# Layer 2's attention set-up: keys and queries from one product, six diffusions made ahead, first blocks' first sums by VectorE

## The chip, the cores and the metric

One core of one Trainium2 chip runs the whole four-layer network in one launch. The metric is the time of one execution in device microseconds (us). Engines: PE is the matrix engine (TensorE), PEld its weight loads, DVE VectorE, ACT ScalarE, POOL GpSimd, SP SyncE.

## The reference, cut to what matters

Layer 2 gets X (4096 x 256) and S (the 0/1 adjacency). It takes two steps; each makes a nucleus (top-p) attention and a diffusion, and then multiplies both by small weights:

```python
def top_p_attention(X, W1, W2, W3):
    q = X @ W1.T @ W2.T            # 4096 x 64
    k = X @ W3.T                   # 4096 x 64
    probs = softmax(q @ k.T)       # 4096 x 4096
    ...                            # keep the largest until their sum reaches 0.9
    return A / max(A.sum(-1), 1e-12)
R = (S + I) / row sums
for n in range(2):
    A  = top_p_attention(Xa, W1, W2, W3)
    Xf = R @ Xf                    # diffusion
    Xa = A @ Xa                    # attention
    Z  = Z + Xf @ U1[n].T + Xa @ U2[n].T
h = X + Z                          # then a layer norm with gain and shift
```

## The kernel before

Rows are worked in 32 blocks of 128. For a block, `scores` makes the logits (PE) and their exponentials (ACT) into one of three large buffers `e`, guesses the cut and takes a first sum above it; `nucleus` searches the cut on VectorE and masks the exponentials; `attention` transposes the masked block and multiplies it by X; `diffuse` multiplies the adjacency by X; `close` applies the small weights. `work` and `psum` are buffer pools; the kernel's builder orders the instructions of each engine itself, from the program order and the buffers.

```python
# keys(src), one group of four blocks; ps_tp has two PSUM buffers
for g in range(NB // 4):
    self.transposed(psum, work, src[:, 4 * g:4 * g + 4, :], None, out=xT)
    pk = ...; matmul(pk, w3 twice, xT)                 # keys, 2 products of 512 columns (L711)
    nc.vector.tensor_copy(kT[half, ...], pk[half, :])
    pq = ...; matmul(pq[:A], w1, xT)                   # queries, first half of the chain (L718)
    nc.scalar.copy(q1, pq[:A])
    pr = ...; transposes of kT                         # keys by rows (L722)
    pq = ...; matmul(pq, w2 twice, q1)                 # queries, second half (L727)
    nc.scalar.copy(qs[:, g * 512:(g + 1) * 512], pq)
# ... moments of the keys (L732)
for b in range(NB):                                    # the spreads: 32 rounds (L737)
    matmul(pg[:, :2 * A + 1], qs[:A, block b], mom)
    nc.scalar.copy(g, pg[:, :2 * A + 1])
    nc.vector.tensor_copy(mean[:, b:b + 1], g[:, 2 * A:])
    nc.vector.scalar_tensor_tensor(..., accum_out=hvar[:, b:b + 1])
# ... (cut)

# in scores(b): the first sum, on ACT
for s in range(2):
    for i, f in ((0, AF.Relu), (2, AF.Sign)):
        nc.scalar.activation(ja, e[:, s * HALF:(s + 1) * HALF], f, bias=nc1, accum_out=fs[:, i + s:i + s + 1])

# the order of the blocks, once per step
keys(X)
for b in range(-2, NB):
    if b >= 0:
        attention(att[:, 0], stage.pop(b)[0], rs.pop(b))
        close(step, b, (twos.pop(b), att))
    if b + 2 < NB:
        stage[b + 2] = scores(b + 2, ABOVE[step])
    if 0 <= b + 1 < NB:
        rs[b + 1] = nucleus(*stage[b + 1], evals=1 + step)
        diffuse(dif[:, 0], b + 1)
        # ... (in step 0 the diffusion is split and stored for step 1)
```

## Time and profile before

| | before |
|---|---|
| median of the runs beside the changed kernel | 5093.11 us (5086.0 to 5099.69, 4 runs) |
| profiled execution | 5087.6 us, mean granted PE clock 0.953 |
| layer 1's last product ends | 2077 us |
| step 0 of layer 2 ends (last attention scaling) | 3363 us |
| step 1 ends | 4734.5 us |
| DVE's first search starts in step 0, step 1 | 2202.2, 3477.2 us |

The windows of the whole steps serve as a ledger: length, then busy us of PE, PEld, DVE, ACT, POOL (with the number of instructions), then granted clock, DMA share and GB/s.

```profile
2078.00:3363.00 1285.00, 1204.81 (x5320) 855.43 (x5320) 971.81 (x2800) 802.55 (x1927) 0.86 (x2) 0.97 0.24 77
3363.00:4734.50 1371.50, 1222.11 (x5332) 858.71 (x5332) 1173.36 (x3494) 861.39 (x2148) 64.37 (x124) 0.96 0.23 72
```

Step 0 is PE's (idle 80 of 1285 us), step 1 is shared: DVE works 1173 and PE 1222 of 1371.5. In rows of PE, one product of the code is often two records (the two products of L711 are `x4`).

### The profile page before, as it was taken

Reading aid. Unit: us, or ns where it says so; the run is one execution under the profiler, and the core shown is the slowest. Engines: PE = TensorE matmul, PEld = TensorE weight load, DVE = VectorE, ACT = ScalarE, POOL = GpSimd, SP = SyncE. Lnnn points to the kernel's source line nnn. Section 1 sums busy time; section 2 is a strip of 40 time slices with the busy share of each in tenths; the row PEclk is TensorE's granted clock in tenths of the full one; section 3 lists DMA queues with packets and bytes.
Section 4 is the critical chain, followed back from the end, with each engine's and each line's share of the span. In section 5 each row is a group of like instructions: output and inputs, shape, how many; then the busy total and the mean of one; then the engine's idle time right before and its main releaser. Section 6 shows DMA issues by size and latency. Waiting matters only on the chain. (4 is left out here: it accounts for less than half of the span.)

```text
span 5087.6 us, 72483 instructions
## 1 busy us (share of the span) xinstructions
PE 4404.3 (87%) x25899; PEld 3464.9 (68%) x25900; DVE 3399.8 (67%) x8018; ACT 2871.7 (56%) x5755; POOL 458.5 (9%) x807
## 2 busy tenths in 40 slices
PE   6799977776777489969999999995999989989799
PEld 4699967776777378547767767753666666666677
DVE  4422228887888722377878787836989999899322
ACT  4333349997999410276666666636676676665111
POOL 3344420000000121000000000000000000000000
PEclk6899989998999799979999999997999999999899
DMA  4499982233232259502222222241112211211566
GB/s 151 158 337 348 340 330 96 96 102 141 96 102 96 80 163 309 181 24 89 69 88 69 88 69 88 71 163 39 62 62 62 80 62 61 81 62 60 183 228 201
DMA packets 338490, 659.76 MB, mean 130 GB/s; under 512 B 74048, under 2 KB 150720, under 8 KB 328896
## 3 DMA queue, kind: packets, MB, share of 16 engines
q1 hardware_dynamic: 189824, 436.29, 26.2%
q10 hardware_dynamic: 117568, 117.98, 7.0%
q0 software_dynamic: 30720, 100.69, 5.2%
q8 instruction: 209, 3.42, 0.3%
q14 instruction: 169, 1.38, 0.1%
HBM read 490.46 MB, written 164.36 MB: 129 GB/s over the span
## 5 line engine op out<-in xcount | busy, mean ns | idle before, releaser
L1073 PE MATMUL ps_a<-X,aT 128*128 128x256 f32 x4096 | 970.6, 390 | 52.3 <-ACT aT L1070 52.2
L1073 PEld LDWEIGHTS ps_a<-X,aT 128*128 128x128 f32 x4096 | 768.2, 192 | 308.4 <-ACT aT L1070 167.2
L254 PE MATMUL acc<-gm,gt 128*128 128x198 bf16 x8192 | 745.9, 250 | 255.4 <-DVE gt L249 243.8
L247 ACT ACTIVATE sg<-lpb,lc 128x1024 bf16<-128x1024 f32 x832 | 870.9, 1135 | 119.4 <-DVE gt L249 78.9
L254 PEld LDWEIGHTS <-gt 128*128 128x128 bf16 x8192 | 692.2, 98 | 308.9 <-DVE gt L249 286.4
L385 PE MATMUL pz<-src,ar 128*128 128x264 f32 x4096 | 549.7, 294 | 48.7 <-ACT src L342 34.1
L249 DVE TENSOR_TENSOR gt<-sg,na 128x4096 bf16<-128x4096 bf16 x208 | 474.2, 2286 | 164.2 <-ACT sg L247 164.2
L385 PEld LDWEIGHTS pz<-src,ar 128*128 128x128 f32 x4096 | 522.9, 194 | 70.3 <-ACT src L342 44.6
L143 PE MATMUL ps_r<-XD,adj_piece 128*128 128x512 f32 x2048 | 501.7, 397 | 29.6 <-DMA adj_piece<-adjs 28.9
L1070 ACT COPY aT<-ps_tp 128x512 f32<-128x512 f32 x512 | 276.8, 583 | 420.9 <-PE ps_tp L1068 413.7
L822 ACT ACTIVATE ja<-e,nc 128x2048 bf16<-128x2048 f32 x256 | 511.0, 1996 | 1.0 <-DVE e L959 0.4
L143 PE MATMUL ps_adj<-XD,adj_piece 128*128 128x512 f32 x2048 | 494.2, 399 | 16.1 <-DMA adj_piece<-adjs 11.0
L764 PE MATMUL ps_logit<-kT,q 64*128 64x512 f32 x1024 | 442.2, 654 | 53.3 <-ACT e L768 51.1
L143 PEld LDWEIGHTS ps_r<-XD,adj_piece 128*128 128x128 f32 x2048 | 382.2, 189 | 131.4 <-DMA adj_piece<-adjs 50.2
L143 PEld LDWEIGHTS ps_adj<-XD,adj_piece 128*128 128x128 f32 x2048 | 385.4, 190 | 99.2 <-DVE XD L115 11.7
L852 DVE SCALAR_TENSOR_TENSOR v<-e,c 128x4096 bf16<-128x4096 f32 x96 | 429.5, 4474 | 1.1
L76 POOL TENSOR_SCALAR ln_var<-ln_mv 128x1 f32<-128x1 f32 (+1 forms) x144 | 49.5, 344 | 4139.3 <-DVE kept L935 1469.6
L959 DVE SCALAR_TENSOR_TENSOR e<-e,edge 128x256 f32<-128x256 f32 x1024 | 415.8, 479 | 1.4
L377 ACT ACTIVATE nb<-a 128x512 bf16<-128x512 f32 x256 | 158.1, 630 | 348.8 <-DMA a<-in_adjt_dram 255.6
L912 DVE MAX8 cand<-v 128x8 f32<-128x256 f32 x1024 | 349.1, 412 | 3.4
L1068 PE MATMUL ps_tp<-ident,e 128*128 128x128 f32 x2048 | 274.3, 276 | 52.9 <-DVE e L959 52.9
L1068 PEld LDWEIGHTS ps_tp<-ident,e 128*128 128x128 f32 x2048 | 242.9, 142 | 90.9 <-DVE e L959 61.9
(285 smaller groups left out, 4869.8 us busy)
## 6 DMA issues: line engine op xcount, KB each, us to landing
adj_piece<-adjs SPq DMA_DIRECT2D x256, 512.0 KB, 5.5
adj_piece<-adjs SPq DMA_DIRECT2D x512, 256.0 KB, 3.5
a<-in_adjt_dram SPq DMA_DIRECT2D x256, 256.0 KB, 5.7
adjs<-ar POOLq DMA_DIRECT2D x256, 256.0 KB, 5.6
na<-nad SPq DMA_DIRECT2D x64, 1024.0 KB, 6.4
nad<-nb POOLq DMA_DIRECT2D x128, 256.0 KB, 5.1
lpb<-lpd ACTq DMA_DIRECT2D x32, 512.0 KB, 5.0
gmd<-gb ACTq DMA_DIRECT2D x64, 198.0 KB, 2.1
```

Source lines behind the costliest of these rows:

```text
L143: nc.tensor.matmul(ps, a[:, k, :], rhs(jc).rearrange("p s d -> p (s d)"), start=(jc == 0 and own is None), stop=(jc == self.NB - 1))
L247: nc.scalar.activation(sg[:, k, :], lpb, AF.Sign, bias=lc[:, jc, h:h + 1])
L249: nc.vector.tensor_tensor(*flat, ALU.is_gt)
L254: nc.tensor.matmul(acc[:, q, :6 * C1], gt[:, k, q * P:(q + 1) * P], gm[:, jc, hh, :], start=(jc == 0 and q % 2 == 0), stop=(jc == NB - 1 a ...
L385: nc.tensor.matmul(pz[q][:, t, :W], ar[:, q, k, :], src[:, jc, t, s], start=(jc == 0 and s == 0), stop=(jc == NB - 1 and s == 1))
L764: nc.tensor.matmul(pl[:, s, :], q[s * A:(s + 1) * A, :], kT[s * A:(s + 1) * A, c * 512:(c + 1) * 512], start=True, stop=True)
L822: nc.scalar.activation(ja, e[:, s * HALF:(s + 1) * HALF], f, bias=nc1, accum_out=fs[:, i + s:i + s + 1])
L852: nc.vector.scalar_tensor_tensor(junk, e, c, e, op0=ALU.is_ge, op1=ALU.mult, accum_out=S)
L912: nc.vector.max(cand[:, 8 * j:8 * j + 8], v[:, k * 256:(k + 1) * 256])
L959: nc.vector.scalar_tensor_tensor(ec, ec, edge[:, j:j + 1], ec, op0=ALU.is_ge, op1=ALU.mult)
L1068: nc.tensor.transpose(pt[:, k * P:(k + 1) * P], e[:, jc * P:(jc + 1) * P], self.ident)
L1073: nc.tensor.matmul(pa[:, :D], aT[:, k * P:(k + 1) * P], X[:, jc, :], start=(jc == 0), stop=(jc == NB - 1))
```

## The change

Its intent: PE does less for the keys, and the work that waits nowhere else (the diffusions) is moved to where PE stood idle, between the keys and block 0's attention.

```diff
 # one-time: W1 and W2 multiplied into one weight, keys and queries side by side in wkq
+for c in range(2):
+    matmul(pt[:, :A], w1[:, c, :], aw2)
+    for s in range(2):
+        nc.vector.tensor_copy(wkq[:, c, s, 1 - s, :], pt[:, :A])
+        nc.vector.tensor_copy(wkq[:, c, s, s, :], aw3[:, c, :])
 # the 32 additions of the layer norm's shift leave the start of step 0 ...
-    nc.vector.tensor_add(xl, X[:, b, :], lnb)
-    nc.scalar.dma_start(xd[b, :, 2, :], xl)
 # ... and go into step 0's closes
+    nc.vector.tensor_add(xb[:, 1], xb[:, 0], affine)
+    nc.scalar.dma_start(xd[at(b), :, 2, :]..., xb[:, 1])
 # the splits of X for step 0's diffusions: from ahead of the keys to behind them
-    self.split(XD[:, b], X[:, b, :])        # at the start
+    self.split(XD[:, b], X[:, b, :])        # after keys(X), if step == 0
 # keys (kT is now centred at their end, ahead of the spreads and not after them)
-    pk from w3, pq from w1, q1, pq from w2 (above)
+    matmul(pk, wkq[:, c, s], xT)            # keys in one half, queries in the other
+    nc.vector.tensor_copy(kT[half, ...], pk[half, :])
+    here = qs[other, g * 512:(g + 1) * 512]
+    nc.scalar.copy(here, pk[other, :])
 # spreads: four blocks to a PSUM bank, the mean taken out of the moments beforehand
-for b in range(NB): ...
+for g in range(NB // 4):
+    four matmuls into pg
+    nc.scalar.copy(t, pg[:, :, :A])
+    nc.vector.tensor_mul(t, t, pg[:, :, A:])
+    nc.vector.tensor_reduce(hvar[:, 4 * g:4 * g + 4], t, AX.X, ALU.add)
 # first sum
+if b < 2:
+    S1 = evaluate("S1", e, c1)              # one DVE instruction over 4096
+else: (ACT, as before)
 # order
+found = keys(X)
+e = scores(0)
+spreads(*found)
+stage = {0: guessed(e, 0, ABOVE[step])}
+rs = {0: nucleus(*stage[0], evals=1 + step)}
+for k in range(EARLY):                      # EARLY = 6
+    if k in (2, 4):
+        stage[k // 2] = guessed(scores(k // 2), k // 2, ABOVE[step])
+    nc.scalar.dma_start(ahead[k], diffusion(step, k)[:, 0])
 # blocks 0 to 5 load their diffusion from ahead; later blocks make it as before
```

## The prediction

> **What bounds the kernel now.** The page's busy shares (PE 87%, DVE 67%, ACT 56%) average four layers, and its chain of waits reaches back over only 6% of the span, all in layer 3. So I read layer 2 by stretches. In the trace, layer 1's last product ends at 2078 us, the first pass of layer 2 (step 0) ends at 3363, the second (step 1) near 4740. I cut each pass into its head (to the end of block 0's attention) and a long middle of 24 blocks.
>
> The windows view; columns after the length are busy us of PE, PE weight loads, DVE, ACT, POOL, then the granted PE clock, DMA share and GB/s:
>
> ```profile
> 2078.00:2255.00 177.00, 125.80 (x494) 69.25 (x495) 93.98 (x331) 90.97 (x219) 0.86 (x2) 0.82 0.20 67
> 2469.00:3333.00 864.00, 839.46 (x3756) 609.98 (x3754) 695.23 (x1934) 571.82 (x1373) 0.00 (x0) 1.00 0.25 79
> 3363.00:3545.00 182.00, 123.67 (x505) 64.72 (x505) 84.00 (x301) 92.35 (x233) 0.00 (x0) 0.84 0.33 108
> 3775.00:4702.00 927.00, 853.01 (x3744) 616.42 (x3745) 862.33 (x2530) 608.62 (x1522) 51.89 (x96) 0.98 0.21 67
> ```
>
> Per block, by division by 24: step 0 takes 36.0 us, of which PE works 35.0 and DVE 29.0, so PE bounds it. Step 1 takes 38.6 us, DVE works 35.9 and PE 35.5, so DVE bounds it with PE just behind. The heads are different: 177 and 182 us, with PE idle for 51 and 58.
>
> The timeline of PE shows where the idle lies. First step 0, then step 1:
>
> ```profile
> 2199.91 3.60 PE L764 MATMUL ps_logit<-kT,q 64*128 64x512 f32 x8 [10.13 <-ACT e L768]
> ...
> 2216.34 3.78 PE L764 MATMUL ps_logit<-kT,q 64*128 64x512 f32 x8 [9.80 <-ACT e L768]
> 2232.89 1.97 PE L1068 MATMUL ps_tp<-ident,e 128*128 128x128 f32 x8 [12.76 <-DVE e L959]
> ```
>
> ```profile
> 3523.73 1.97 PE L1068 MATMUL ps_tp<-ident,e 128*128 128x128 f32 x8 [26.56 <-DVE e L959]
> ```
>
> PE waits for exponentials that stand behind the first sums on ACT, then for the first mask (L959). And one group of the keys, of eight:
>
> ```profile
> 3385.16 1.93 PE L718 MATMUL ps_tp<-e,aw 128*64 128x512 f32 x4
> 3387.02 0.46 PE L722 MATMUL ps_tp<-ident,kT 64*128 64x64 f32 x4
> 3387.41 0.45 PE L732 MATMUL ps_a<-e 128*64 128x65 f32 x4
> 3387.82 1.12 PE L727 MATMUL ps_tp<-e,aw 64*128 64x512 f32 x2
> 3388.87 0.65 PE L96 MATMUL ps_tp<-ident,X 128*128 128x128 f32 x4
> 3389.45 0.45 PE L732 MATMUL ps_a<-e 128*64 128x65 f32 x4
> 3389.83 0.66 PE L96 MATMUL ps_tp<-ident,X 128*128 128x128 f32 x4
> 3390.32 2.02 PE L711 MATMUL ps_tp<-e,aw 128*128 128x512 f32 x4
> ```
>
> PE has no gap there: the keys are PE-bound at 7.1 us a group (the group before starts L711 at 3383.21).
>
> [...] granted clock 0.82 and 0.84 in the heads, 1.00 in step 0's middle. [...] the trace has DVE standing at L1084 behind an unfinished diffusion for 95.4 us in step 0's middle.
>
> **The change part by part.**
>
> *Keys and queries from one product.* W1 and W2 are multiplied once, so L718 and L727 go: from the starts above, 1.86 us (3385.16 to 3387.02) and 1.05 us (3387.82 to 3388.87) a group. 7.1 - 2.9 = 4.2 us a group; over 8 groups 23 us per step, all on the path. Copies per group stay below that: ACT three at 0.58 us, DVE 0.68 and 0.42. The one-time product costs some transposes and small copies, about 3 us, while step 0 waits for weights anyway.
>
> *Removed at the start of step 0.* The 32 additions of the shift with their stores go into step 0's closes. In the trace ACT's first key copy came at 2093.65, after such a store, 13 us after its transposes. I count 5 us of earlier start. The price is one DVE addition (0.42 us) and one store per block in step 0, where DVE has 7 us of room a block.
>
> *Spreads.* Before: 32 products, each with its ACT copy of 0.27 and three small DVE instructions, took from 2157.3 to 2174.5, 17 us; in step 1 3434.0 to 3451.5. After: four blocks share a bank, eight rounds. A round is four products at 0.32 us (L737's x4 rows, two products in 0.64 us), 1.3 us: about 11 us, so 6 saved. The scores of block 0 are put ahead of them in program order, but its exponentials need one of the three large buffers, and all three are the keys' scratch until the spreads have read it. Only the first products into PSUM can go ahead, so I count no more than the shorter spreads and the earlier centring of kT.
>
> *First sums by DVE for blocks 0 and 1.* Four ACT passes of 2.0 us plus readouts (2189.1 to 2198.3, 9.2 us) become one DVE instruction of 4.47 us (the row of L852). For block 0 both are on the path: 4.5 saved, and block 1's passes no longer delay its exponentials.
>
> *Six diffusions ahead.* One costs (182.6 + 11.7) / 24 = 8.1 us of PE, from the middle's rows of L143 and L137. One already ran beside the keys. So five more, 40 us of PE, move from the first blocks into the hole.
>
> *Step 0's sum*, by PE, since PE bounds it from the keys on. Work removed: 23 + 6 = 29. Idle removed: the head had 51; I leave 20 (8 while weights land, 3 while kT is centred, 9 between diffusions, which share one PSUM bank), so 31. Together 60 us. DVE does not get in the way: with masks starting some 50 us earlier and 28.5 us a block it stays ahead of PE's 27 us blocks plus backlog.
>
> *Step 1's sum*, by DVE. Its first search started at 3477.2. After: keys end 23 earlier; from keys to the first exponential 21.1 us become about 16; from there to the first search 22.6 become about 14.5 (exponentials 5, Z and first cut 4, DVE's sum 4.7, second cut 0.8). So the search starts 36 us earlier. DVE then carries one first sum more (4.5) and saves idle: it stood idle about 5 us in 3477:3545 and about 20 us in the ten blocks to 3775 where PE was the reason. I count 12 of these. 36 - 4.5 + 12 = 44 us.
>
> 60 + 44 = 104 us. I take off 6 for friction that such a reordering has had no chance to tune out: **98 us, 4998 us**.
>
> **The rivals.**
> 1. *Diffusions stall on their one bank.* Each must be read out by ACT and then DVE (L1083, L1084) before the next begins, and DVE may be inside a pass of 4.47 us. For: the 95.4 us above. Against: PE has three blocks' logits (7 us each) to put between. If every gap is 4 us longer, 24 us a step come back: about 5045.
> 2. *Diffusions stand in front of the first attention.* About 90 us of PE work (logits 21, spreads 11, diffusions 49, gaps 9) follow the keys, while the first mask is ready after about 50. Then block 0's large buffer is freed late and block 3's scores with it. In step 0 this costs nothing, PE being busy; in step 1 DVE would run dry between blocks 2 and 3, for 10 to 20 us: about 5012.
> 3. *The new stores hold ACT.* [...] Against: ACT waits for transposes 213 us in step 0's middle, 9 us a block, so it has room. If 1 us a block reaches PE: about 5030.
> 4. *Better:* PE has almost no idle left after the keys, and with the diffusions gone from blocks 1 to 5 step 1 runs at DVE's 36 us: some 25 us more, 4973.
>
> **Range and chances.** The key saving is nearly certain, and rivals 1 to 3 can hardly all strike. 8 in 10: 4960 to 5042. The 2% line lies at 4994, four us under my figure, so it is close to even: faster 0.45, within 2% 0.53, slower 0.02.
>
> **What would show it.** L711 rows 4 to 4.5 us apart in the keys; no L718 or L727. First L959 mask some 50 us earlier after each step's start. L143 rows of six diffusions between the keys and the first L1068, with PE gaps under 3 us, and the granted clock near 1.0 there. Blocks 1 to 5 of step 0 some 28 to 30 us apart by the attention's scaling, of step 1 about 36. It is wrong if the holes are filled yet the first attentions start no earlier, if DVE waits at L1084 inside the first search, or if blocks beyond the sixth grow longer than 36.0 and 38.6 us.

## More of the kernel before

In step 1 the blocks do not come evenly: their lengths repeat with a period of nine, from about 34 to about 46 us. The order of PE's rows in the trace shows what goes with it: in seven blocks of nine the diffusion stands ahead of the block's transposes, then once after seven of the eight transposes of the first round, then once after all eight (the 34 us block), and then it is in front again and the long blocks come.

## The result, and the profile after

The changed kernel takes 5002.82 us in the median (4998.48 to 5005.48, 4 runs) against 5093.11 for before. The ratio is 0.9822, 95% interval 0.9805 to 0.9839. (Ratios here are the mean time of one kernel's runs over that of the other's of the same rounds, so not quite the ratio of the medians.) That is "within 2%" at the edge, and 5 us from the predicted 4998. (The prediction's 98 us and 4998 us belong to a before of 5096; against the 5093 measured here the gain is 90 us.) A second set of runs, the unaltered kernel run again later, gave 5000.18 us and 0.9819 (0.9806 to 0.9832). All outputs are right.

The same ledger of the changed kernel:

```profile
2078.00:3307.40 1229.40, 1181.06 (x5282) 848.21 (x5282) 977.22 (x2736) 776.99 (x1878) 0.86 (x2) 0.99 0.25 81
3307.40:4646.60 1339.20, 1203.16 (x5288) 864.66 (x5288) 1182.72 (x3421) 836.23 (x2092) 67.93 (x124) 0.96 0.23 75
```

Step 0 is 55.6 us shorter: PE works 23.8 less (1204.81 - 1181.06) and is idle 31.9 less (80.2 against 48.3). Step 1 is 32.3 us shorter: DVE works 9.4 more and is idle 41.7 less (198.1 against 156.5). The rest of the program is 3 us shorter.

The windows of the head and middle of step 0, and of the head of step 1, to be set beside those of before:

```profile
2078.00:2225.00 147.00, 128.07 (x621) 87.60 (x622) 92.46 (x240) 68.47 (x180) 0.86 (x2) 0.95 0.45 138
2225.00:2377.00 152.00, 140.53 (x613) 99.13 (x611) 132.61 (x379) 103.07 (x249) 0.00 (x0) 0.97 0.08 24
2420.00:3282.00 862.00, 850.57 (x3768) 615.99 (x3767) 700.39 (x1946) 564.07 (x1356) 0.00 (x0) 1.00 0.26 83
3307.00:3473.00 166.00, 136.78 (x628) 97.70 (x626) 104.75 (x266) 70.17 (x185) 0.00 (x0) 0.89 0.59 189
```

The head of step 0 ends 30 us earlier with 19 us of PE idle (the prediction left 20) and the granted clock at 0.95 instead of 0.82. Blocks 1 to 5 then take 152 us, five at 30.5, where they took 178. From block 7 on the middle is as before, 36 us a block.

The keys of step 1, one group of eight, in PE's timeline (start, length, line, and in brackets the idle time before and who ended it):

```profile
3337.16 1.98 PE L725 MATMUL ps_tp<-e,wkq 128*128 128x512 f32 x4
...
3340.53 1.09 PE L96 MATMUL ps_tp<-ident,X 128*128 128x128 f32 x8 [0.16 <-ACT e L729]
3341.46 0.40 PE L740 MATMUL ps_a<-e 128*65 128x65 f32 x4
3341.91 1.98 PE L725 MATMUL ps_tp<-e,wkq 128*128 128x512 f32 x4
3343.74 0.40 PE L740 MATMUL ps_a<-e 128*65 128x65 f32 x4
3344.69 0.46 PE L732 MATMUL ps_tp<-ident,kT 64*128 64x64 f32 x4 [0.55 <-DVE kT L727]
```

A group takes 4.76 us, not 4.2: two rows now carry a wait, 0.55 us for VectorE's copy of the keys and 0.15 us for ACT's copy of the queries. In the group of before that the prediction shows there was none.

The spreads of the changed kernel, from their first to their last product, in step 0 and in step 1 (the windows view):

```profile
2139.98:2149.15 9.17, 9.17 (x70) 7.96 (x67) 5.40 (x14) 2.61 (x7) 0.00 (x0) 1.00 0.09 29
```

```profile
3363.90:3377.55 13.65, 13.65 (x66) 13.65 (x68) 5.89 (x14) 2.60 (x7) 0.00 (x0) 0.50 0.65 233
```

PE has no gap in either; what differs is the granted clock, 1.00 and 0.50. It fell in step 1 from 1.00 to 0.50 at 3361 us, at the end of the keys; the longest wait in the 34 us before was 0.55 us.

The end of the hole in step 0, then the same place in step 1:

```profile
2194.09 0.50 PE L137 MATMUL ps_r<-XD,identr 128*128 128x512 f32 x1 [2.03 <-DVE dif L1115]
2194.43 7.50 PE L143 MATMUL ps_r<-XD,adj_piece 128*128 128x512 f32 x32
2203.09 1.62 PE L1099 MATMUL ps_tp<-ident,e 128*128 128x128 f32 x8 [1.16 <-DVE e L990]
```

```profile
3436.96 0.44 PE L1099 MATMUL ps_tp<-ident,e 128*128 128x128 f32 x2 [0.93 <-DVE e L990]
...
3444.51 2.07 PE L1104 MATMUL ps_a<-X,aT 128*128 128x256 f32 x4 [4.20 <-ACT aT L1101]
3446.20 0.81 PE L137 MATMUL ps_r<-XD,identr 128*128 128x512 f32 x1
3446.81 8.92 PE L143 MATMUL ps_r<-XD,adj_piece 128*128 128x512 f32 x32
3455.57 2.75 PE L1104 MATMUL ps_a<-X,aT 128*128 128x256 f32 x12
```

In step 0 the waits for the first mask (12.76 us before) and between diffusions have become 1 to 2 us. In step 1 the wait of 26.56 us has become 0.93, but then two things stand inside block 0's attention: a wait of 4.20 us for ACT, which was in its four half passes of block 2's first sum, and the sixth diffusion, 9.4 us long. So although the first mask comes 31.2 us earlier in the step, block 0's attention ends only 16.4 us earlier; the following five blocks then run at 34.6 us each (before 38.0) and recover 17 more, and block 6, where diffusions return, costs 48.6 us and gives 9 of them back.

The rows after such waits show one thing more. `L1104` x16 takes 3.72 us in its usual state. After waits in the changed kernel, and then at the first of these places in its second run:

```profile
2409.18 3.72 PE L1104 MATMUL ps_a<-X,aT 128*128 128x256 f32 x16 [1.80 <-ACT aT L1101]
...
3895.03 3.72 PE L1104 MATMUL ps_a<-X,aT 128*128 128x256 f32 x16 [3.06 <-ACT aT L1101]
...
4242.66 6.64 PE L1104 MATMUL ps_a<-X,aT 128*128 128x256 f32 x16 [3.57 <-ACT aT L1101]
```

```profile
2408.48 5.41 PE L1104 MATMUL ps_a<-X,aT 128*128 128x256 f32 x16 [1.80 <-ACT aT L1101]
```

In the changed kernel the sixteen products took 3.72 us after 3.06 us of idle and 6.64 us after 3.57 us, where the trace has a granted clock of 0.50 from 4242.7 to 4246.0 us. But the length of the wait just before does not settle it: the same 1.80 us left the rate in one run of the kernel and not in the other. Over layer 2 in the traces of before and of the changed kernel, such rows of sixteen took 3.72 us after each of the 14 waits of 1.34 to 1.98 us, 5.38 us after one of 2.68 us, and 5.1 to 6.7 us after each of the six waits of 3.19 us or more; but also 5.10 and 5.87 us after waits of 1.22 and 0.81 us. After the waits of 2.68 us and more, the slower rows cost 1.4 to 3.0 us beside the wait itself; what decides was not studied.

### The profile page after: what moved, and what is told of

Same layout as the page of the kernel before. It is cut to its first block, busy times and chain, and to the rows that moved or that the text cites. A ratio compares the mean times of both kernels' runs of the same rounds, so it can differ in the third digit from the quotient of the medians.

```text
span 4996.8 us, 72143 instructions
## 1 busy us (share of the span) xinstructions
PE 4366.1 (87%) x25817; PEld 3469.1 (69%) x25818; DVE 3415.4 (68%) x7880; ACT 2819.7 (56%) x5645; POOL 461.8 (9%) x807
## 5 line engine op out<-in xcount | busy, mean ns | idle before, releaser
L1104 PE MATMUL ps_a<-X,aT 128*128 128x256 f32 x4096 | 975.4, 391 | 62.8 <-ACT aT L1101 62.3
L1104 PEld LDWEIGHTS ps_a<-X,aT 128*128 128x128 f32 x4096 | 771.0, 193 | 321.9 <-ACT aT L1101 177.7
L385 PE MATMUL pz<-src,ar 128*128 128x264 f32 x4096 | 553.6, 296 | 48.6 <-ACT src L342 34.8
L860 ACT ACTIVATE ja<-e,nc 128x2048 bf16<-128x2048 f32 x240 | 478.9, 1996 | 0.8 <-DVE e L990 0.6
L787 PE MATMUL ps_logit<-kT,q 64*128 64x512 f32 x1024 | 448.9, 646 | 12.9 <-ACT e L791 12.6
L806 DVE SCALAR_TENSOR_TENSOR v<-e,c 128x4096 bf16<-128x4096 f32 x100 | 447.4, 4474 | 3.7 <-ACT c L834 2.8
L1099 PE MATMUL ps_tp<-ident,e 128*128 128x128 f32 x2048 | 276.7, 276 | 35.3 <-DVE e L990 35.2
L939 DVE SCALAR_TENSOR_TENSOR v<-e,hi 128x2048 f32<-128x2048 f32 x128 | 301.1, 2352 | 2.2
```

Source lines behind the costliest of these rows:

```text
L385: nc.tensor.matmul(pz[q][:, t, :W], ar[:, q, k, :], src[:, jc, t, s], start=(jc == 0 and s == 0), stop=(jc == NB - 1 and s == 1))
L787: nc.tensor.matmul(pl[:, s, :], q[s * A:(s + 1) * A, :], kT[s * A:(s + 1) * A, c * 512:(c + 1) * 512], start=True, stop=True)
L806: nc.vector.scalar_tensor_tensor(junk, e, c, e, op0=ALU.is_ge, op1=ALU.mult, accum_out=S)
L939: nc.vector.scalar_tensor_tensor(v, ec, hi, ec, op0=ALU.is_lt, op1=ALU.mult, accum_out=sb[:, s:s + 1])
L1104: nc.tensor.matmul(pa[:, :D], aT[:, k * P:(k + 1) * P], X[:, jc, :], start=(jc == 0), stop=(jc == NB - 1))
```

## The experiments

Layers 0 and 1 are the same code in all kernels, yet layer 1's last product ended between 2070 and 2087 us over the profiled executions. So step 0 is counted below from its own first keys product, and step 1 from the end of step 0; both ends are the last attention scaling of the step. Times of the profiled executions, in us:

| kernel | step 0: block 0 | block 10 | end | step 1: block 0 | block 10 | end | blocks 11 to 28 against changed | median of runs | ratio to before (95%) |
|---|---|---|---|---|---|---|---|---|---|
| before | 160.2 | 519.1 | 1268.3 | 182.4 | 571.8 | 1371.4 | +33.3 | 5093.1 | 1 |
| changed | 131.8 | 469.1 | 1214.4 | 166.0 | 533.8 | 1339.2 | 0 | 5002.8 | 0.9822 (0.9805-0.9839) |
| changed, again | 131.3 | 467.6 | 1211.1 | 166.3 | 535.4 | 1342.3 | +3.8 | 5000.2 | 0.9819 (0.9806-0.9832) |
| no diffusion ahead | 128.1 | 487.8 | 1235.3 | 153.2 | 543.3 | 1347.1 | +2.4 | 5025.2 | 0.9871 (0.9856-0.9886) |
| first sums on ACT | 140.3 | 475.7 | 1223.1 | 173.9 | 542.8 | 1354.1 | +9.2 | 5020.6 | 0.9868 (0.9853-0.9883) |
| old keys | 159.9 | 513.8 | 1259.2 | 175.9 | 547.0 | 1359.6 | +15.5 | 5061.9 | 0.9941 (0.9926-0.9956) |
| spreads first | 127.3 | 464.5 | 1209.6 | 166.4 | 534.1 | 1341.0 | +2.4 | 4993.0 | 0.9813 (0.9800-0.9826) |
| keys and spreads only | 138.1 | 497.9 | 1251.3 | 166.2 | 555.6 | 1352.7 | +16.8 | 5048.2 | 0.9920 (0.9905-0.9935) |
| five in step 1 | 127.4 | 464.0 | 1209.7 | 159.0 | 531.7 | 1343.9 | +0.1 | 5002.1 | 0.9826 (0.9813-0.9840) |
| five, third sum on DVE | 127.6 | 460.3 | 1212.9 | 148.8 | 527.7 | 1340.8 | -4.4 | 5000.1 | 0.9825 (0.9810-0.9840) |
| four in step 1 | 127.0 | 463.6 | 1210.2 | 158.2 | 523.8 | 1333.0 | -9.3 | 4991.1 | 0.9806 (0.9793-0.9819) |
| four, keys staggered | 130.3 | 471.2 | 1215.6 | 153.0 | 520.1 | 1327.9 | -13.3 | 4997.8 | 0.9814 (0.9800-0.9828) |
| old keys, five in step 0 | 151.4 | 495.6 | 1242.4 | 175.1 | 546.1 | 1355.3 | +12.9 | 5044.3 | 0.9912 (0.9896-0.9927) |
| three in step 1 | 127.7 | 464.9 | 1209.8 | 152.0 | 526.9 | 1340.7 | -7.1 | 5002.3 | 0.9821 (0.9808-0.9835) |

The two profiles of the changed kernel differ by 3.3 us in step 0 and 3.1 us in step 1, and the two runs with old keys, whose step 1 is the same code, by 4.3 us in step 1. Differences of that size in the table mean nothing. The rounds ran on different chips, each beside runs of before (medians 5088.3 to 5093.1), so kernels of different rounds are better compared by their ratios.

A single mark in step 1 depends on where a kernel stands in its nine-block rhythm. The column "blocks 11 to 28 against changed" takes that out: it is how much later than in the changed kernel a block ends, in the mean over two whole turns (the two turns agree within 1.5 us). It is computed from the same attention scalings. The sections below use it beside the step's end, which counts for the total time.

The theory after the first comparison: the gain is work taken from PE (keys) plus idle filled (diffusions), as predicted; step 1 falls short because the sixth diffusion stands in the attention. The main rival: the moved diffusions are worth little, and in step 1 they cost as much as they save.

**No diffusion ahead.**

```diff
-EARLY = min(6, NB)
+EARLY = 0
-for k in range(EARLY):
+for k in range(max(EARLY, 5)):      # scores of blocks 1 and 2 stay early
-    nc.scalar.dma_start(ahead[k], diffusion(step, k)[:, 0])
+    if k < EARLY:
+        nc.scalar.dma_start(ahead[k], diffusion(step, k)[:, 0])
```

> The changed kernel with no diffusion ahead: each stands again beside its own block; keys, spreads, first sums and the early scores of blocks 1 and 2 stay as changed. Theory A (the prediction's): the diffusions fill idle of PE in step 0, about 31 us, and save DVE some 12 us in step 1: 5003 + 40, so 5035 to 5050, and the loss lies about 3:1 on step 0. Theory B (rival 2 at work in step 1): they fill the hole of step 0 but stand in front of the first attention of step 1, whose end they delay as much as they save: 5003 + 25, so 5020 to 5032, all of it in step 0, while step 1 gets no longer or even shorter.

Measured: 5025.15 us. Step 0 is 20.9 us longer than the changed kernel's, step 1 7.9. The total is theory B's, the split at the end is theory A's (about 3:1). Step 1's first attention ends 12.8 us earlier without the diffusions, as rival 2 said, yet the step ends later. From block 7 to 29 the two kernels lead in turn, this one from 11 us earlier to 15 us later, and over whole turns it is 2.4 us later, which is noise. So in step 1 the diffusions ahead are not shown to save anything: they cost about as much as they save, as theory B had it. The two heads of this kernel, to the end of block 0's attention:

```profile
2076.00:2219.50 143.50, 94.28 (x456) 61.13 (x457) 91.06 (x237) 65.07 (x172) 0.86 (x2) 0.81 0.18 52
3327.00:3480.00 153.00, 96.70 (x462) 65.78 (x463) 88.91 (x207) 64.52 (x175) 0.00 (x0) 0.79 0.41 129
```

The heads are only 3.5 and 13 us shorter than those of the changed kernel although they hold five diffusions less each, and the clock is at 0.81 and 0.79. So nearly all of what step 0's five diffusions need was free.

**First sums on ACT.**

```diff
-if b < 2:
+if b < 0:
     S1 = evaluate("S1", e, c1, bufs=3)
```

> The changed kernel with the first sums of blocks 0 and 1 on ACT again (four half passes of about 2.0 us each). Theory A: both sums lay on the path to the first search, 4.5 us a step and some more for block 1's exponentials: 5003 + 9 to 15, so 5012 to 5018. Theory B: in step 0 PE is full with diffusions anyway (nothing lost, 0 to 3), in step 1 DVE gets back the 4.5 us of block 1 and the net is near zero: 5000 to 5008.

Measured: 5020.59 us, more than either theory said. Step 0 is 8.7 us longer, which is theory A. Step 1 is 14.9 us longer at its end and 9.2 over whole turns; 7.9 of it is there when block 0 ends, so theory A holds there too, and the rest comes and goes with the rhythm. The profile has one place that looks like the cause and is not, block 4 (PE, and then what DVE waited for just before):

```profile
3611.98 1.97 PE L1099 MATMUL ps_tp<-ident,e 128*128 128x128 f32 x8 [24.93 <-DVE e L990]
...
3576.86 0.21 DVE L899 TENSOR_SCALAR d<-d,gw 128x1 f32<-128x1 f32 x1 [6.97 <-ACT gw L891]
```

DVE's search stood 7 us for a 128 x 1 value of ACT's that was given out behind half passes of a first sum (`ja`, 2.0 us each) in ACT's order, and PE then 25 us for the mask; block 4 took 56.1 us instead of 41.5. But blocks 5 and 6 are then 16.7 us shorter together (34.8 and 37.1 us against 40.0 and 48.6), and when block 6 ends this kernel is 8.7 us behind, hardly more than at block 0. A long wait in the middle of a step is a loss only if the marks behind it say so.

**Old keys.** Queries by two products again (`w1k`, `w2k` loaded besides), all else as changed.

```diff
-    nc.scalar.copy(here, pk[other, :])
+    matmul(pq[:A], w1k[:, c, :], xT[:, c, :]); nc.scalar.copy(q1, pq[:A])
     ...
+    matmul(pq, w2k twice, q1); nc.scalar.copy(here, pq[other, :])
```

> The changed kernel with queries by two products as before (by W1, then by W2: four more 512-wide products and one more ACT copy a group), all else as changed. Theory A (the prediction's 23 us a step, all on the path): 5003 + 46, so 5043 to 5052. Theory B: in step 1 the changed keys run at 4.76 us a group and not at 4.2, because the copies of a bank wait for one another, so undoing costs only 7.1 - 4.76 = 2.35 us a group there, 19 us; in step 0 the diffusions fill what idle there is and 23 remain: 5003 + 42 or less, 5030 to 5045, the step 1 part under 20.

Measured: 5061.88 us; step 0 44.8 us longer than the changed kernel's, step 1 20.4. Step 1 is near theory B's "under 20" (15.5 over whole turns). Step 0 is far more than both. (The profile caught the slowest of the four executions, 5078 us; layer 1 ended 9.4 us later in it than in the changed kernel, which counting from the first keys product leaves out.) The keys themselves, first to last product, took 53.3 us there against 38.9, only 14.4 more. The rest is in PE's timeline at block 0's attention:

```profile
2227.79 1.39 PE L1109 MATMUL ps_tp<-ident,e 128*128 128x128 f32 x8
2233.88 0.76 PE L137 MATMUL ps_r<-XD,identr 128*128 128x512 f32 x1 [4.71 <-DVE dif L1125]
2234.44 7.04 PE L143 MATMUL ps_r<-XD,adj_piece 128*128 128x512 f32 x24
2242.76 2.11 PE L143 MATMUL ps_r<-XD,adj_piece 128*128 128x512 f32 x8 [1.28 <-DMA adj_piece<-adjs]
2244.71 3.62 PE L1114 MATMUL ps_a<-X,aT 128*128 128x256 f32 x16
```

With the longer keys the builder put the sixth diffusion between the first transposes and the first attention product of step 0, as it had in step 1 of the changed kernel. This was tested by itself later (below).

**Spreads first.**

```diff
-e = scores(0)
 spreads(*found)
+e = scores(0)
```

> The changed kernel with the spreads ahead of block 0's scores in program order. Theory A (buffer claim of the prediction: all three large buffers are the keys' scratch, so block 0's exponentials cannot start before the last spreads product in either order): no difference beyond 3 us, 5000 to 5006. Theory B: the eight logit products that went ahead in step 0 save time: 5006 to 5012.

Measured: 4993.01 us, against theory A's 5000 to 5006. But layer 1 ended 4.4 us earlier in this profile; in layer 2 itself step 0 is 4.8 us shorter and step 1 1.8 longer. ACT's timeline, first of the changed kernel, then of this one:

```profile
2148.29 0.37 ACT L771 COPY e<-ps_tp 128x256 f32<-128x256 f32 x1 [1.14 <-PE ps_tp L767]
2149.18 1.03 ACT L791 ACTIVATE e<-ps_logit 128x1024 f32<-128x1024 f32 x1 [0.52 <-PE ps_tp L767]
```

```profile
2142.41 0.37 ACT L771 COPY e<-ps_tp 128x256 f32<-128x256 f32 x1 [0.52 <-PE ps_tp L767]
2142.68 1.03 ACT L791 ACTIVATE e<-ps_logit 128x1024 f32<-128x1024 f32 x1
```

In both the first exponential (L791) starts within 0.3 us of the end of the last spreads product (2149.15 and 2142.38 us): the prediction's claim about the three large buffers holds. Putting the scores first therefore brings nothing. It may cost a little: the four kernels with spreads first and otherwise the changed step 0 lie at 1209.6 to 1210.2 us there, the two profiles of the changed kernel at 1214.4 and 1211.1. In total time no difference is shown, the intervals overlap.

**Keys and spreads only.** The loop of before on the changed `keys` and `spreads`, with first sums on ACT and no diffusion ahead.

```diff
+spreads(*found)
+for b in range(-2, NB): (as in the kernel before)
-e = scores(0) ... (the changed order)
-if b < 2:
+if b < 0:
```

> The changed kernel with the loop of before (no diffusion ahead, scores of block 2 after the attention of block 0) and first sums on ACT: so only the one-product keys, the shorter spreads and the moved shift are left. Theory A (the prediction's terms): step 0 gains 5 + 23 + 6 = 34 us, step 1 23 + 6 = 29, 63 in all against before, ratio 0.988. Theory B (step 1's keys gave 17 and not 23, and its spreads 13.4 us and not 11): step 0 gains 28 to 32, step 1 18 to 22, about 50 in all, ratio 0.990.

Measured: 5048.23 us, 0.992, 41 us against before: less than both theories. Counted from the first keys product step 0 gains 17.0 us; 2.1 more are the earlier start (17.6 us from layer 1's last product to the first keys product before, 15.5 here). So it is 19 us where A said 34. Step 1 gains 18.7 where B said 18 to 22 (16.5 over whole turns). The ledger of step 0, its head, and then its last two blocks, of before and of this run:

```profile
2075.60:3341.90 1266.30, 1195.68 (x5282) 859.00 (x5282) 969.49 (x2732) 794.86 (x1902) 0.87 (x2) 0.97 0.25 78
...
2075.00:2229.00 154.00, 102.66 (x458) 68.11 (x457) 82.66 (x234) 82.91 (x196) 0.87 (x2) 0.76 0.17 48
```

```profile
3301.14:3363.03 61.89, 57.25 (x280) 46.53 (x280) 38.83 (x110) 25.34 (x61) 0.00 (x0) 1.00 0.22 69
```

```profile
3273.34:3341.92 68.58, 59.22 (x280) 47.75 (x280) 43.85 (x134) 25.36 (x62) 0.00 (x0) 0.98 0.20 66
```

Of the 29 us that A gave to keys and spreads 12 are missing, half in the head and half in the last two blocks. In the head PE works 23.1 us less (125.80 - 102.66), about what has left; block 0's attention ends 22.1 us earlier and block 29 23.7. That is nearly the whole 23 us of the keys, though PE is idle 51 us in the head as before and its clock is lower, 0.76 (before 0.82). The spreads gave nothing: they take 16.7 us as before, without a gap of PE, but at half clock:

```profile
2133.79:2150.52 16.73, 16.73 (x72) 14.62 (x70) 5.89 (x14) 2.60 (x7) 0.00 (x0) 0.50 0.01 1
```

That fits one reading, which no run tested by itself: with products taken out of a stretch that waits anyway, its granted clock is lower (0.76 against 0.82 in the head), and those that stay take longer (the spreads 16.7 us at 0.50, where the changed kernel has 9.2 us at 1.00). Then the last two blocks take 68.6 us instead of 61.9, with PE idle for 9.4 instead of 4.6, and 6.7 us are lost again. Over the whole step PE's busy sum falls by only 9.1 us (1204.81 - 1195.68), but most of the rest is no sign of slower products: blocks 1 to 29 show 12 us more of it than before, at a clock of 1.00 in both and no greater length.

**How many ahead in step 1.** Spreads first in all of these; six ahead in step 0, five, four or three in step 1.

```diff
-EARLY = 6
+EARLY = (6, 5)[step]        # then (6, 4), (6, 3)
```

> Spreads first, and in step 1 five diffusions ahead instead of six (six in step 0). In the instruction order the sixth stood inside block 0's attention of step 1; now it is beside block 5. Theory A (rival 2: it held the attention, and that was what step 1 lost): block 0's attention of step 1 ends 8 to 10 us earlier and the step 6 to 9 us, 4984 to 4988. Theory B (step 1 is bound by VectorE, whose work and first search are the same): the attention ends earlier, but the step by less than 3 us, 4990 to 4996.

> As the run with five, with four ahead in step 1. Theory A (PE's work ahead delays the first attention): a further 0 to 3 us less than the run with five. Theory B (the holes between the first blocks of step 1 are long enough for any of them): within 3 us of the run with five. Theory C (each diffusion that stays with its block costs VectorE-bound blocks some wait): 3 to 6 us more than the run with five.

> As the run with four, with three ahead in step 1. Theory A (fewer ahead is better as long as the first masks are not ready): within 3 us of the run with four. Theory B (a middle number is best: none ahead gave a step 1 of 1347 us, four 1333, six 1341): 2 to 8 us more than the run with four. Theory C (the end of step 1 depends on where the rhythm of its blocks happens to stand, and not on the number): anything from 1330 to 1348 us for step 1, with no order among the numbers.

Measured: 5002.13, 4991.11 and 5002.29 us. With five the first attention of step 1 ends 7.4 us earlier than with six (159.0 against 166.4), because the sixth no longer stands in it, but the step ends no earlier (1343.9 against 1341.0): theory B of that run. At the end of block 10 the numbers are in order: none 543.3 (without spreads first), three 526.9, four 523.8, five 531.7, six 534.1. Over whole turns it is nearly the same order: four and three are 9.3 and 7.1 us earlier than the changed kernel, five 0.1, six and none 2.4 later. So in these profiles, one of each kernel, a middle number is best by about 10 us over six and over none. At the end of the step this does not show: none 1347.1, three 1340.7, four 1333.0, five 1343.9, six 1341.0. Between block 10 and the end lie 21 blocks, two turns of the nine-block rhythm and three blocks over, and those took between 797 us (keys and spreads only) and 814 us (three). In the medians four is 11 us under five and three 11 over four, past what the theories of these runs gave, but for theory C of the last. Four is the lowest of all, but its interval overlaps that of the changed kernel, so in total time it is not shown to be better.

**Third first sum on DVE** (five ahead in step 1).

```diff
-if b < 2:
+if b < 3:
     S1 = evaluate("S1", e, c1, bufs=3)
```

> As the run with five, and the first sum of block 2 by VectorE too, so that ACT's four half passes (9 us in step 1) no longer stand before the copies of block 0's attention. Theory A: PE's gap of 4.2 us before the first attention product of step 1 goes, 3 to 5 us less than the run with five. Theory B: VectorE gets 4.5 us more in each step; in step 1, where it is the bound, that is 4 to 5 us more than the run with five.

Measured: 5000.14 us, equal to the run with five. PE in step 1, with five ahead, and then with the third sum on DVE:

```profile
3445.97 6.50 PE L1104 MATMUL ps_a<-X,aT 128*128 128x256 f32 x16 [4.21 <-ACT aT L1101]
```

```profile
3440.37 3.72 PE L1104 MATMUL ps_a<-X,aT 128*128 128x256 f32 x16 [0.94 <-ACT aT L1101]
...
3485.56 1.97 PE L1099 MATMUL ps_tp<-ident,e 128*128 128x128 f32 x8 [16.67 <-DVE e L990]
```

The wait for ACT and the half speed behind it are gone, and block 0's attention ends 10 us earlier (148.8 against 159.0). Some 4 us of that is an earlier start of the keys. But block 1's mask is then 16.67 us late, and over whole turns 4.5 us are left, little more than the keys' earlier start. Here the work moved to DVE only moved the wait.

**Keys staggered** (four ahead in step 1): the rows of one group of keys are transposed after the next group's product.

```diff
 for g in range(NB // 4):
     ... pk, copies of kT and here
-    transposes of group g, copy to kr
+    if g: transposes of group g - 1, copy to kr
+transposes of the last group, copy to kr
```

> As the run with four, and the keys' transposes of one group of keys are given out after the next group's product, so that PE does not wait for VectorE's copy of the keys. Theory A (that wait of about 0.55 us a group is why step 1's keys run at 4.76 us a group and not at 4.2): 4.2 to 4.3 us a group, 3 to 5 us less in step 1 than the run with four; step 0, where parts of diffusions fill the gap, gains under 2. Theory B (the waits of the copies on one PSUM bank set the pace): still 4.6 to 4.8 us a group, no gain.

Measured: 4997.76 us; in step 1 the groups stand 4.48 to 4.61 us apart, mostly between the two theories.

```profile
3336.20 1.98 PE L735 MATMUL ps_tp<-e,wkq 128*128 128x512 f32 x4
3338.11 0.46 PE L723 MATMUL ps_tp<-ident,kT 64*128 64x64 f32 x4
3338.50 0.45 PE L747 MATMUL ps_a<-e 128*65 128x65 f32 x4
3339.43 1.09 PE L96 MATMUL ps_tp<-ident,X 128*128 128x128 f32 x8 [0.48 <-DVE e L725]
```

The wait for the copy of the keys is gone, and in its place PE waits 0.48 us for DVE's copy of the transposed rows to free a `ps_tp` buffer, of which there are two. So the 0.55 us was a wait for a copy of 0.69 us, as theory A had it, but a group uses the two buffers four times, and the next copy in the line takes its place. Step 1 gains 5 us on the run with four, 3.1 of them because its keys start earlier in the step (11.9 us after step 0's end against 15.0), and step 0 loses 5. The runs fall into two groups, 4985 and 4986 us and then 4998 to 5004 us, so nothing is shown to come of it.

**Old keys, five in step 0.**

```diff
+EARLY = (5, 6)[step]        # on the run with old keys
```

> The run with old keys, with five diffusions ahead in step 0 instead of six (six in step 1). There the sixth stood between the first transposes and the first product of block 0's attention in step 0. Theory A (that position, not the keys, was what held step 0 so long: 44.8 us more than the changed kernel against 14 to 23 from the keys themselves): block 0's attention of step 0 ends 10 to 14 us earlier and step 0 is 10 to 20 us shorter, near 1240 to 1249 from its first keys product; 5042 to 5052 in all. Theory B (PE is full in step 0, so the diffusion costs the same wherever it stands): the attention ends earlier, the step stays within 5 us of 1259; 5057 to 5062.

Measured: 5044.32 us; step 0 is 16.8 us shorter than with six (1242.4 against 1259.2), step 1 within 4.3. Theory A for the step; block 0's attention came 8.5 us earlier where it said 10 to 14. One diffusion fewer ahead is faster by 17.6 us in the median (the runs do not overlap; the intervals of the ratios just touch, 0.9926 and 0.9927), since PE now goes from the transposes to the attention (after a wait of 4.22 us for ACT):

```profile
2214.92 1.48 PE L1109 MATMUL ps_tp<-ident,e 128*128 128x128 f32 x8
2220.62 5.27 PE L1114 MATMUL ps_a<-X,aT 128*128 128x256 f32 x16 [4.22 <-ACT aT L1111]
```

So rival 2 is a real danger, in the step where the prediction thought it harmless. The old keys then still cost 28.0 us in step 0 against the changed kernel, where the prediction gave them 23 (one diffusion fewer is ahead here).

**The changed kernel again.** No edit.

> The changed kernel unaltered, so that the runs beside it can be set against it on one chip, and to see how far the untouched layers 0 and 1 move its profile. All theories: ratio to before 0.981 to 0.984; step 0 from its first keys product 1212 to 1217 us, step 1 1335 to 1343 us.

Measured: 5000.18 us, ratio 0.9819, step 0 1211.1 (one us under the expected range) and step 1 1342.3. It shows how far the marks in the table move by themselves.

## Why the prediction was right, and where it was not

The total was right to 5 us, and the class too; the parts less so, and part of the agreement is luck. Of the 104 us in the sums, step 0 gave 56 of 60 and step 1 32 of 44; 6 us of unexplained "friction" and the few us of the rest of the program cover some of the difference. Three stages of experiments split the gain: before to keys and spreads only, to no diffusion ahead (which adds first sums on DVE, early scores and the new order of the loop), to the changed kernel. Step 0 is read when block 29 ends, step 1 over whole turns of the rhythm; the values at the step's end stand in brackets. (The prediction's 31 us of idle in step 0 are parted as in the run with keys and spreads only: 5 to the earlier start, 26 to the rest.)

| part | predicted, step 0 | measured | predicted, step 1 | measured |
|---|---|---|---|---|
| earlier start | 5 | 2 (2) | | |
| keys, spreads | 29 | 23.7 (17.0) | 29 | 16.5 (18.7) |
| first sums on DVE, early scores, new order | 26 with the next | 8.8 (16.0) | 15 with the next | 14.4 (5.6) |
| diffusions ahead | | 20.3 (20.9) | | 2.4 (7.9) |
| sum | 60 | 55 (56) | 44 | 33.3 (32.2) |

- **Bounds.** Right. Step 0 in PE's ledger: work 29 predicted, 23.8 measured; idle 31 predicted, 31.9 measured. The head's idle was to be 20 and is 19. (PE's busy sum moved by 12 us in blocks that did not change, above, so these two agree no better than that.)
- **Keys.** In step 0 the 23 us came (block 0's attention 22.1 us earlier with keys and spreads only). In step 1 2.35 us a group was saved, not 2.9 (7.11 to 4.76): the sum counted PE's rows alone and called the copies hidden. They are in time, but a group's chain through two `ps_tp` buffers exposes 0.55 and 0.15 us. The last product of the keys (L732, now L740) ends 17.2 us earlier in the step instead of 23. Half of what is missing comes before the keys: their first product starts 14.9 us after step 0's end where it was 12.0, after a wait of 9.63 us for loads instead of 6.76; why, no run shows. This is the term that was mis-sized most clearly.
- **Spreads.** 11 us expected; step 0 has 9.2 at a granted clock of 1.00, step 1 13.7 at 0.50 (and step 0 16.7 at 0.50 with keys and spreads only), each without a gap of PE. So the size went with the granted clock, though not with it alone (13.7 and 16.7 us, both at 0.50); the prediction left it out of this term. The claim that exponentials cannot go ahead of them is confirmed.
- **Earlier start.** 5 us expected; from layer 1's last product to the first keys product 15.5 us instead of 17.6, so 2.
- **First sums.** 4.5 us expected in step 0, and block 1's exponentials no longer delayed. When the sums alone go back to ACT, 8.7 us are lost in step 0 and, over whole turns, 9.2 in step 1. That is all of the 8.8 us that this stage gave up to block 29 of step 0; the 16.0 at the end hold also the 7 us that the last two blocks lost with keys and spreads only.
- **Diffusions.** All idle removed was given to them together with the other parts; taken out alone they cost 20.9 us in step 0, and in step 1 7.9 at the end but 2.4 over whole turns, which is noise. Between them PE waited at most 2.4 us in both steps, so **rival 1** fell. **Rival 2** happened in step 1, as predicted: the sixth stands in block 0's attention. Its end moves 7.4 us when it is taken out, but the step's end does not; fewer ahead, four, is 10 us better at block 10 and over whole turns. **Rival 3** left no trace that was found: the new stores took 2.7 us in the median from issue to landing, and blocks in step 0's middle keep their 36 us. **Rival 4** did not happen.
- **First masks.** "Some 50 us earlier" was wrong: 29.8 and 31.2. In step 0 the search starts 35.3 us earlier, but block 1's first sum on DVE (4.5 us) then stands inside it, and it lasts 5.5 us longer (35.7 against 30.2 us).
- **Step 1.** The search started 29 us earlier in the step and not 36: the keys are 6 us short, the way from them to the first exponential 3 (the spreads), and from there to the search it is 1.5 us better than expected. DVE works 9.4 us more, about both its first sums. At the end of block 29 the changed kernel is 41 us ahead, which looks like the predicted 44, and at the end of the step 32; both are marks in the rhythm, and over whole turns it is 33.3. The last two blocks take 73.3 us against 64.4. There the changed kernel is at another place of the nine-block rhythm: its 34.3 us block is number 29, so the longer one that follows it is number 30 of 31; before, the last two blocks are short ones. That the rhythm comes from the instruction order goes with all the traces but no run took it away, so it is not shown. Nor is it the only reading of the last two blocks: the two kernels with the old loop take 64.4 and 63.4 us in them, the twelve profiles with the new one 67.3 to 75.0, so the new order itself may be the cause.

The splits of X, which the change moved behind the keys in step 0, were not tested by themselves; they are in every run but before.

## What to carry to other kernels

Filling a hole went with a higher clock here: with the diffusions in it the head of step 0 had a granted clock of 0.95 and without them 0.81, and it was only 3.5 us longer for five diffusions of about 8 us each. The clock was also lost without a long wait: the same spreads took 9.2 us at 1.00 in step 0 and 13.7 us at 0.50 in step 1, where no wait in the 34 us before was longer than 0.55 us. Do not take a total that comes out as proof of its terms; build the change up in stages, and read each stage at several marks. The last two blocks of a step gave or took 7 us here, and a rhythm of nine blocks moved the lead of one kernel over another by up to 26 us, so that a long block in a profile was no loss and the end of a step no measure of a part; a mean over whole turns was. And count which instruction stands next in each engine's order after every edit: one diffusion at the wrong place in it cost 17 us.
